# Sharing the unpacking of 4-bit weights anew among three stages of a fused attention and feed-forward kernel

## The chip, the cores and the metric

The kernel runs on one core of a Trainium2 chip. The metric is the device time of one execution in microseconds; the time of a kernel is the median of its runs. The profile is that of one execution, with its own time.

## The reference

The input x has 2 batches of 1024 tokens of 1024 values. It is normalised, and two branches read the result: attention with 32 query heads and 8 key heads of 32 values, causal, with rotary positions; and a gated feed-forward layer of inner width 2752, whose weights come packed as 4-bit numbers with a zero point and a scale for each group of 128 rows. Cut to what matters:

```
xn = layernorm(x)
q, k, v = xn @ wq, xn @ wk, xn @ wv          # q and k are then rotated
s = softmax(causal(q @ k.T / sqrt(32))) @ v @ wo
gate, up = split(xn @ dequant(qweight_gu))   # 1024 x (2 * 2752)
f = (silu(gate) * up) @ dequant(qweight_down)
out = x + s * silu(f)
```

`dequant` is scale times (number minus (zero point + 1)).

## The kernel before

Attention is done for one batch after the other, then the feed-forward layer for both. The order of stages is: layer norm of batch 0; then for each batch a projection to queries, keys and values (`project`), attention (`attend`) and the output projection (`project_out`); then the feed-forward part. The layer norm of batch 1 runs inside the first output projection.

**Unpacking.** TensorE needs the packed weights as floating-point integers. They are unpacked once, written to device memory, and read from there by the feed-forward part. A unit of gate and up is a block of 128 columns of both matrices; there are 22, and the last has 64 columns. The down matrix gives 12 more units. `unpack` is a Python generator that records the instructions of its units in small steps, so that another stage can record them between its own. A unit is four loads on SP's queue (two of packed words, L242, two of zero points, L244), on VectorE an AND (L258), a shift with an AND (L260) and two additions (L263), on ScalarE two conversions to float (L267), and two stores on POOL's queue (L249, 512 KB each). Each `next` on the generator is one turn. It gives one turn for the first load, four for each unit and one for the last store, so n units need 4n + 2 turns. A unit's loads are recorded one unit ahead, and its stores one unit behind.

**Who drives the generator.** Before the change three stages do:
- The first output projection has units 0 to 7, 34 turns. It takes three turns at the start of each part from the eighth of its 14 parts on (21 turns), and the rest after the loop.
- The projection of batch 1 has units 8 to 19, 50 turns. Its inner function `turned` takes three turns after each block of 512 tokens, and there are 20 blocks: 4 of the keys and 16 of the queries.
- The second output projection has units 20 and 21 and the 12 of the down matrix, 58 turns. It takes three turns in each of its 14 parts, 42, and the rest after the loop.

**A block in the projection.** `turned` makes a block of queries or keys with 8 products (L384), and VectorE reads the PSUM bank twice: once times a cosine (L388), once with neighbours swapped (L390). POOL multiplies by the sine and adds (L391, L392). ScalarE then rounds the sum to the high half (L394), VectorE subtracts it for the low half (L396), and SP stores both halves (L397, L398). After each pair of blocks of queries the normalised input is split in the same way (ScalarE L439, VectorE L440) and stored (L441, L442). The turns of `unpack` are recorded under `behind(turn)`, which puts their instructions behind the rotation's last ones.

From the third block pair on, the projection also makes the score products of the first head group (L554, with a mask, L548), whose maximum VectorE takes from PSUM (L564). They use two PSUM banks. After each half of these rows come eight small steps on VectorE (L586 to L591) and four transposes on TensorE (L599), which need them.

**The order of the work.** The stages up to the attention, and the output projection, are recorded in program order, and a scheduler then orders the instructions of each engine; in the attention and in the last product of the feed-forward part the order is written by hand. Each engine executes its own queue in order. So an instruction that waits holds back all that stand behind it on that engine. SP's queue carries nearly all loads and most stores; POOL's carries the stores of unpacked weights and half of those of the output projection, and also the two steps of the rotation.

An output projection has 14 parts in its loop, each 16 products of 128x256 into a PSUM bank (L880), of six in turn. VectorE copies the bank of even parts, ScalarE that of odd ones (L892), and POOL or ScalarE stores the copy (L893). The second output projection runs behind the loads of the whole normalised input (L946) and of the first weights (L937) on SP's queue.

Of the kernel before, what the change touches and what calls it, by code (L numbers as in the profile page):

```python
# [36 lines left out]
def block_kernel(  # L37
# [19 lines left out]
    B, T, D = x.shape  # L57
# [4 lines left out]
    NF = -(-INTER // P)  # L62
# [146 lines left out]
    def look(pool, psp):  # L209

        bad = pool.tile([P, 4], F32, name="bad")
        nc.vector.memset(bad, 0.0)
        yield from survey(pool, bad, sc_gu, qz_gu, gi_gu, z_gu, 0, "gu")
        yield from survey(pool, bad, sc_d, qz_d, gi_d, z_d, 2, "d")
        for g in range(G_GU):
            r0 = g * (P // G_GU)
            r1 = r0 + P // G_GU
            nc.scalar.dma_start(zb_gu[r0:r1], z_gu[g : g + 1].to_broadcast([r1 - r0, 2 * INTER, 2]))
        yield
        for g in range(G_D):  # L220
            r0 = g * 16
            r1 = r0 + 16 if g < G_D - 1 else RD
            nc.scalar.dma_start(zb_d[r0:r1], z_d[g : g + 1].to_broadcast([r1 - r0, D, 2]))
        yield
        scales_turned(pool, psp)
        yield
        one = pool.tile([P, 1], F32, name="one")
        nc.vector.tensor_reduce(one, bad, AX.X, ALU.add)
        ps = psp.tile([1, 1], F32, name="ps_bad", tag="ps")
        nc.tensor.matmul(ps, one, ones_f[:, :1], start=True, stop=True)  # L230
        nc.vector.tensor_scalar(flag, ps, 1.0, None, ALU.min)
        yield
# [126 lines left out]
    def project(b, xnT, w_k, qs, ks, v, side, head):  # L359


        with tc.tile_pool(name="qkv_w", bufs=3, reuse_waits="tile") as wp, tc.tile_pool(name="qkv", bufs=3, reuse_waits="tile") as pool, tc.tile_pool(
# [9 lines left out]
            def behind(turn):  # L372

                order = ExitStack()
                for i in turn:
                    order.enter_context(tc.issue_after(i.ins))
                return order

            def turned(w, dst, work=iter(()), blocks=range(NB)):
                for n in blocks:  # L380
                    tok = slice(n * TB, (n + 1) * TB)
                    ps = psp.tile([P, TB], F32, name="ps_qk")
                    for s in range(NS):
                        nc.tensor.matmul(ps, w[:, s, :], xnT[:, s, tok], start=(s == 0), stop=(s == NS - 1))  # L384
                        if s % 2:
                            next(work, None)
                    t1 = pool.tile([P, TB], F32, name="rot1")
                    nc.vector.tensor_tensor(t1, ps, cs[:, 0, tok], ALU.mult)  # L388
                    t2 = pool.tile([P, TB], F32, name="rot2")
                    nc.vector.stream_shuffle(t2, ps, swap)  # L390
                    nc.gpsimd.tensor_tensor(t2, t2, cs[:, 1, tok], ALU.mult)  # L391
                    turn = [nc.gpsimd.tensor_tensor(t1, t1, t2, ALU.add)]  # L392
                    hi = pool.tile([P, TB], F32R, name="rot_hi", bufs=2)
                    turn.append(nc.scalar.copy(hi, t1))  # L394
                    lo = pool.tile([P, TB], F32R, name="rot_lo", bufs=2)
                    turn.append(nc.vector.tensor_tensor(lo, t1, hi.bitcast(F32), ALU.subtract))  # L396
                    nc.sync.dma_start(dst[0, :, tok], hi.bitcast(F32))  # L397
                    nc.sync.dma_start(dst[1, :, tok], lo.bitcast(F32))  # L398
                    with behind(turn):
                        for _ in range(3 if b else 1):  # L400
                            next(side, None)
                return turn

# [1022 lines left out]
    def start_ffn(stack):  # L1426

        xp = stack.enter_context(tc.tile_pool(name="xs", bufs=1, side="right"))
        xs = [xp.tile([P, NS, T], F32R, name=f"x_{t}") for t in range(2)]
        for _ in activations(xs, 0):  # L1430
            pass
        ring = itertools.cycle([xp.tile([P, D], F32R, name=f"w_{i}") for i in range(6)])
        ws = {(f, u): load_gu(ring, f, u) for f, u in ((0, 0), (0, 1), (1, 0))}
        return xs, ring, ws

    def open_x():
        st = ExitStack()
        xp = st.enter_context(tc.tile_pool(name="x", bufs=1, side="right", reuse_waits="tile"))
        return st, xp.tile([P, NS, T], F32, name="xnT"), xp
# [7 lines left out]
    for b in range(B):  # L1447
        keep_open = ExitStack()
        keep = keep_open.enter_context(tc.tile_pool(name="keep", bufs=1, reuse_waits="tile"))
        oT = keep.tile([P, NS, T], F32, name="oT")  # L1450
        q0_open = ExitStack()
        q0p = q0_open.enter_context(tc.tile_pool(name="at_q0", bufs=1, reuse_waits="tile"))
        with tc.tile_pool(name="at_first", bufs=1, reuse_waits="tile") as fp, tc.tile_pool(
            name="qkv_T", bufs=1, reuse_waits="tile"
        ) as qp:

            room = [q0p.tile([P, T], F32R, name=f"room_{j}") for j in range(1 + 2 * NREP)]
            v = qp.tile([P, NT, N_KV * HD], F32, name="v")
            with tc.tile_pool(name="ps_s", bufs=1, space=PSUM, reuse_waits="tile") as ps_s:
                head = Maxima(qs_dram[b], ks_dram[b], fp, ps_s, room)  # L1460
                if b == 0:
                    with tc.tile_pool(name="prep", bufs=1) as pool, tc.tile_pool(
                        name="prep_ps", bufs=1, space=PSUM
                    ) as psp:
                        first = look(pool, psp)
                        project(b, xnT, w_k, qs_dram[b], ks_dram[b], v, first, head)
                        for _ in first:
                            pass
                else:
                    with tc.tile_pool(name="unpack", bufs=2, side="right", reuse_waits="tile") as up:  # L1470
                        side = unpack(up, range(8, 20), False)
                        project(b, xnT, w_k, qs_dram[b], ks_dram[b], v, side, head)
                        for _ in side:
                            pass
                x_open.close()
                output = Output(b, oT, q0p)
                attend(head, v, oT, output)
        if b == B - 1:
            ffn_args = start_ffn(ffn_open)
            xnT = xp = None  # L1480
        else:
            x_open, xnT, xp = open_x()
        with tc.tile_pool(name="unpack", bufs=3, side="right", reuse_waits="tile") as up:
            side = unpack(up, range(8) if b == 0 else range(20, NF), b == B - 1)
            w_k = project_out(output, side, 3, xnT, xp)
            for _ in side:
                pass
        q0_open.close()
        keep_open.close()
# [57 lines left out]
```

## Time and profile before

| | us |
|---|---|
| median of 3 runs | 2293.89 (2293.84 to 2294.37) |
| the profiled execution, its own time | 2293.33 |
| its span, from the first to the last instruction | 2291.6 |
| TensorE busy in the span | 2239.3 (98%) |
| VectorE busy | 1420.2 (62%) |
| ScalarE busy | 1132.3 (49%) |
| POOL busy | 792.4 (35%) |

The stages around the change in that execution, in us from the start of the span:

| stage | from | to |
|---|---|---|
| first output projection, alone on TensorE but for the transposes of the layer norm | 562 | 668 |
| projection of batch 1 | 668 | 853 |
| attention of batch 1 | 853 | 1191 |
| second output projection, alone on TensorE | 1191 | 1290 |
| feed-forward part | 1290 | 2292 |

A row of the profile's timeline gives the start, the duration, the engine, the line, the operation, what it writes and reads, how many instructions are merged into it, and in brackets how long the engine had stood idle before it and for what. On TensorE a float32 product counts as two records. PE is TensorE, DVE is VectorE, ACT is ScalarE. "Granted clock" (PEclk) is the share of full clock that TensorE was given; it is 1.00 in all stages named here.

### The profile page before, as it was taken

What the parts mean: (1) busy time and instruction counts of PE and PEld (TensorE: products, weight loads), DVE (VectorE), ACT (ScalarE), POOL (GpSimd) and SP (SyncE); (2) the same over time, 40 slices, a digit from 0 to 9 for tenths busy, and PEclk for the clock granted to TensorE, in tenths of its full rate; (3) what the DMA queues carried; (4) which work ended last, traced back from release to release, by engine and by line L of the source; (5) the groups of instructions that cost most, each with busy time, mean ns of one, the idle gap of its engine ahead of it and who ended that gap; (6) DMA issues with size and microseconds to landing.
All of it is one profiled execution on the core that took longest, in us unless ns stands there. A gap on an engine that the chain in (4) does not pass through costs nothing.

```text
span 2291.6 us, 30825 instructions
## 1 busy us (share of the span) xinstructions
PE 2239.3 (98%) x11313; PEld 1537.5 (67%) x11313; DVE 1420.2 (62%) x2268; ACT 1132.3 (49%) x1819; POOL 792.4 (35%) x569
## 2 busy tenths in 40 slices
PE   7989999999999999999999999999999999999998
PEld 4455555555874465555558888888877888888875
DVE  5544677773324736777722367667877777777775
ACT  2102544553223325445533455555887555556875
POOL 1303677774035427776741100000234100001362
PEclk9999999999999999999999999999999999999999
DMA  5727323122468971231319623231846655323475
GB/s 180 220 91 244 80 47 93 38 75 76 129 210 280 301 215 47 52 88 38 80 54 344 181 56 83 55 83 55 303 138 219 176 137 139 96 71 105 137 231 154
DMA packets 262183, 309.50 MB, mean 135 GB/s; under 512 B 19147, under 2 KB 197707, under 8 KB 261880
## 3 DMA queue, kind: packets, MB, share of 16 engines
q1 hardware_dynamic: 245172, 260.62, 38.4%
q0 software_dynamic: 10752, 38.02, 5.2%
q10 hardware_dynamic: 6100, 8.82, 1.2%
q8 instruction: 91, 1.49, 0.3%
q14 instruction: 68, 0.56, 0.1%
HBM read 214.58 MB, written 97.03 MB: 136 GB/s over the span
## 4 chain that ended last, share of the span: by engine, by line
PE 82%; issue 7%; POOL 6%; DVE 2%; ACT 2%; DMA 1%; SPq 0%; ACTq 0%; POOLq 0%; DVEq 0%
PE acc L1198 27%; PE acc L1079 12%; PE ps_wo L880 10%; PE st L661 7%; PE s L554 7%; PE o L708 5%; PE ps_qk L384 5%; PE l L726 3%; PE st L676 2%; PE ps_v L407 1%; POOL rot L391 1%; PE s L548 1%; POOL rot L392 1%; POOL p L821 1%; ACT p L686 1%
## 5 line engine op out<-in xcount | busy, mean ns | idle before, releaser
L1198 PE MATMUL acc<-x,w 128*128 128x512 f32 x2752 | 640.1, 393 | 1.2 <-ACT gate L1169 0.9
L1198 PEld LDWEIGHTS acc<-x,w 128*128 128x128 f32 x2752 | 512.3, 188 | 120.5 <-DVE h L1171 7.2
L564 DVE TENSOR_REDUCE mx<-s 128x1 f32<-128x512 f32 (+3 forms) x672 | 384.8, 608 | 190.3 <-PE s L554 91.7
L968 DVE TENSOR_SCALAR acc<-acc,r_gu 128x1024 f32<-128x1024 f32 x301 | 389.1, 1293 | 166.5 <-PE acc L1198 164.9
L686 ACT ACTIVATE p<-st 128x512 f32<-128x512 f32 (+3 forms) x768 | 314.7, 497 | 316.8 <-PE st L676 314.6
L966 ACT ACTIVATE acc<-acc,r_gu 128x1024 f32<-128x1024 f32 x301 | 327.4, 1088 | 231.5 <-PE acc L1198 226.7
L1182 POOL TENSOR_TENSOR h_lo<-h,h_hi 128x512 fp32r<-128x512 f32 x78 | 100.3, 1287 | 805.2 <-DVE h L1160 300.6
L821 POOL TENSOR_TENSOR p<-p 128x2048 f32<-128x2048 f32 (+3 forms) x122 | 360.0, 2955 | 9.0 <-PE o L708 4.6
L968 DVE TENSOR_SCALAR acc<-acc,r_d 128x512 f32<-128x512 f32 x320 | 241.7, 759 | 62.0 <-PE acc L1079 59.3
L966 ACT ACTIVATE acc<-acc,r_d 128x512 f32<-128x512 f32 x320 | 210.8, 663 | 61.8 <-PE acc L1079 55.0
L384 PE MATMUL ps_qk<-xnT,w_qk 128*128 128x512 f32 x512 | 236.0, 602 | 2.5 <-DVE rot L390 2.5
L880 PE MATMUL ps_wo<-oT,w_o 128*128 128x256 f32 x1024 | 232.1, 382 | 0.0
L1079 PE MATMUL acc<-h_lo,w 128*128 128x512 f32 (+1 forms) x576 | 228.9, 397 | 3.0 <-POOL h_lo L1182 2.6
L1079 PE MATMUL acc<-h_hi,w 128*128 128x512 f32 (+1 forms) x576 | 229.5, 398 | 0.7 <-ACT h_hi L1181 0.7
L880 PEld LDWEIGHTS ps_wo<-oT,w_o 128*128 128x128 f32 x1024 | 191.1, 190 | 40.9 <-issue 16.7
L708 PE MATMUL o<-p,v 128*32 128x512 f32 (+3 forms) x1536 | 162.9, 496 | 0.9 <-POOL p L689 0.9
L384 PEld LDWEIGHTS ps_qk<-xnT,w_qk 128*128 128x128 f32 x512 | 94.6, 192 | 99.8 <-issue 93.4
L689 POOL TENSOR_SCALAR_AFFINE_SELECT p<-p 128x512 f32<-128x512 f32 x128 | 80.5, 636 | 163.5 <-ACT p L686 123.0
L391 POOL TENSOR_TENSOR rot<-rot,cs 128x512 f32<-128x512 f32 x40 | 51.3, 1283 | 239.6 <-DVE rot L390 230.2
L554 PE MATMUL s<-kst,room 128*128 128x512 f32 (+3 forms) x384 | 130.4, 379 | 0.0
L1079 PEld LDWEIGHTS acc<-h_lo,w 128*128 128x128 f32 (+1 forms) x576 | 108.4, 188 | 31.0 <-POOL h_lo L1182 5.4
L1079 PEld LDWEIGHTS acc<-h_hi,w 128*128 128x128 f32 (+1 forms) x576 | 108.3, 188 | 30.6 <-issue 2.9
(163 smaller groups left out, 2405.7 us busy)
## 6 DMA issues: line engine op xcount, KB each, us to landing
w<-ng SPq DMA_DIRECT2D x86, 512.0 KB, 5.2
w<-nd SPq DMA_DIRECT2D x63, 512.0 KB, 4.0
ng<-nf POOLq DMA_DIRECT2D x42, 512.0 KB, 6.9
room<-qs SPq DMA_DIRECT2D x160, 128.0 KB, 4.0
x<-xs SPq DMA_DIRECT2D x32, 512.0 KB, 10.2
qst<-qs SPq DMA_DIRECT2D x96, 128.0 KB, 3.8
xt<-in_L_attn_x SPq DMA_DIRECT2D x16, 512.0 KB, 6.2
w_qk<-in_L_attn_wq SPq DMA_DIRECT2D x16, 512.0 KB, 5.0
```

Source lines behind the costliest of these rows:

```text
L384: nc.tensor.matmul(ps, w[:, s, :], xnT[:, s, tok], start=(s == 0), stop=(s == NS - 1))
L554: nc.tensor.matmul(s[:, c * w : (c + 1) * w], q[j][:, qt * P : (qt + 1) * P], k[:, k0:k1], start=n == 1, stop=c == n - 1 and (n > 1 or not ...
L564: nc.vector.tensor_reduce(mx[:, at, js[0] : js[0] + n, k0 // TB], s[:, : w * n].rearrange("p (j t) -> p j t", j=n), AX.X, ALU.max)
L661: nc.tensor.matmul(s[:, q0:], kst[g][:, kt * P : (kt + 1) * P], stack[g][j][:, qlo + q0 : qlo + TB], start=True, stop=False,)
L686: nc.scalar.activation(p[:, j, q0:], st[j][:, q0:], AF.Exp, scale=1.0 / math.sqrt(HD))
L708: nc.tensor.matmul(o[HD * j : HD * (j + 1), q0:], v[:, kt, HD * g : HD * (g + 1)], p[:, j, q0:], start=(kt == 0), stop=last,)
L821: what(*args)
L880: self.last = nc.tensor.matmul(ps[:, c * self.BLK : (c + 1) * self.BLK], self.ws[c0 + c][:, g, :], self.oT[:, g, t0 : t0 + self.BLK], star ...
L966: nc.scalar.mul(a, a, r)
L968: nc.vector.tensor_scalar(a, a, r, None, ALU.mult)
L1079: nc.tensor.matmul(acc[c], w[:k, c * P : (c + 1) * P], ht[:k, :], start=(f == 0 and t == 0), stop=(t == 1), skip_group_check=(f > 0),)
L1198: nc.tensor.matmul(a[:, n, :], w[i][:, g * P : (g + 1) * P], xs[t][:, g, n * TB : (n + 1) * TB], start=(g == 0 and t == 0), stop=(t == 1), ...
```

## The change

The 22 units of gate and up are shared anew. The first output projection gets units 0 to 10 (11 instead of 8, 46 turns), the projection of batch 1 gets units 11 to 18 (8 instead of 12, 34 turns) and takes two turns a block instead of three, and the second output projection gets units 19 to 21 (3 instead of 2) and the 12 of the down matrix as before (62 turns). The two output projections still take three turns at a time.

```
                     with behind(turn):
-                        for _ in range(3 if b else 1):
+                        for _ in range(2 if b else 1):
                             next(side, None)
...
                     with tc.tile_pool(name="unpack", bufs=2, side="right", reuse_waits="tile") as up:
-                        side = unpack(up, range(8, 20), False)
+                        side = unpack(up, range(11, 19), False)
                         project(b, xnT, w_k, qs_dram[b], ks_dram[b], v, side, head)
...
         with tc.tile_pool(name="unpack", bufs=3, side="right", reuse_waits="tile") as up:
-            side = unpack(up, range(8) if b == 0 else range(20, NF), b == B - 1)
+            side = unpack(up, range(11) if b == 0 else range(19, NF), b == B - 1)
             w_k = project_out(output, side, 3, xnT, xp)
```

## The prediction

> **What bounds the kernel now.** I read the page's busy row first, then the busy time by stretch around the three places that share the unpacking, then TensorE's own waits there, and last the queues that stand behind those waits.
>
> ```profile
> PE 2239.3 (98%) x11313; PEld 1537.5 (67%) x11313; DVE 1420.2 (62%) x2268; ACT 1132.3 (49%) x1819; POOL 792.4 (35%) x569
> ```
>
> TensorE is busy for 98% of the span. A change that adds no matmul can win only what TensorE stands idle, and loses only where it makes TensorE wait anew. So the question is where its 52 us of idle time lie.
>
> ```profile
> core 0: us, PE busy (x) PEld busy (x) DVE busy (x) ACT busy (x) POOL busy (x), PEclk, DMA share, GB/s
> 560.00:668.00 108.00, 108.00 (x543) 94.77 (x536) 34.33 (x83) 31.32 (x49) 20.07 (x26) 1.00 0.68 209
> 668.00:695.00 27.00, 27.00 (x64) 11.96 (x63) 8.64 (x20) 5.60 (x8) 9.25 (x8) 1.00 0.22 71
> 695.00:853.00 158.00, 152.03 (x468) 83.55 (x467) 83.36 (x184) 42.89 (x61) 61.81 (x56) 1.00 0.88 274
> 1165.00:1290.00 125.00, 125.00 (x638) 100.26 (x637) 26.46 (x69) 37.40 (x53) 27.98 (x30) 1.00 0.75 247
> ```
>
> The rows are the first output projection, the start of the second projection, the rest of it, and the second output projection. Both output projections keep TensorE fully busy. All the idle time that the change can reach is in the third row: 158.00 - 152.03 = 5.97 us, 0.26% of the span, with the DMA engines at 0.88. That caps the gain at about 6 us. TensorE's rows with a wait in that stretch are these, the wait in brackets:
>
> ```profile
> 755.68 0.51 PE L554 MATMUL s<-room,room 128*128 128x512 f32 x1 [1.23 <-DVE mx L564]
> 762.19 0.38 PE L599 MATMUL m_ps<-ident_b,mt 128*128 128x128 bf16 x4 [0.62 <-DVE mt L588]
> 782.63 0.50 PE L554 MATMUL s<-room,room 128*128 128x512 f32 x1 [0.99 <-DVE mx L564]
> 790.88 0.44 PE L554 MATMUL s<-room,room 128*128 128x384 f32 x1 [0.19 <-DVE mx L564]
> 800.55 0.50 PE L554 MATMUL s<-room,room 128*128 128x512 f32 x1 [1.38 <-DVE mx L564]
> 820.03 0.38 PE L599 MATMUL m_ps<-ident_b,mt 128*128 128x128 bf16 x4 [1.47 <-DVE mt L588]
> ```
>
> They sum to 5.88 us. Each is a score product (L554) that needs a PSUM bank which a maximum on VectorE (L564) has yet to read, or the transposes (L599) that need the last step after those maxima (L588). VectorE is not full (83.36 of 158 us): the maxima stand in its queue behind something. For the third wait its timeline shows what:
>
> ```profile
> 779.81 0.69 DVE L396 TENSOR_TENSOR rot_lo<-rot,rot_hi 128x512 fp32r<-128x512 f32 x1 [3.06 <-ACT rot_hi L394]
> 780.42 0.29 DVE L260 TENSOR_SCALAR nib<-qw 128x512 uint16<-128x512 uint16 x1
> 780.62 0.69 DVE L440 TENSOR_TENSOR x_lo<-xnT,x_hi 128x512 fp32r<-128x512 f32 x1
> 781.22 0.42 DVE L263 TENSOR_TENSOR nib<-nib,zt 128x512 uint16<-128x512 uint16 x1
> 781.55 0.69 DVE L440 TENSOR_TENSOR x_lo<-xnT,x_hi 128x512 fp32r<-128x512 f32 x1
> 782.16 0.75 DVE L564 TENSOR_REDUCE mx<-s 128x1 f32<-128x256 f32 x2
> ```
>
> After a wait of 3.06 us for the rotation to come back from ScalarE, half a unit (L260, L263) and two splits (L440) run before the maximum that TensorE waits for.
>
> **The change: what a unit costs.** A full unit of gate and up is on VectorE 0.29 + 0.29 + 2 x 0.42 = 1.42 us (L258, L260, L263), on ScalarE 2 x 1.06 = 2.1 us (L267), on POOL 2 x 0.91 = 1.8 us of issuing stores (L249, 512 KB each), on SP four loads of some 0.44 us (L242, L244, 64 KB each). Nothing of it is added or taken away in all; 22 units stay. Three places get other numbers.
>
> **First output projection, 8 to 11 units.** Sums added: VectorE 4.3, ScalarE 6.3, POOL 5.4, SP 5.3 us. Engine time isn't what paces them: the last conversions start at 637.88, 642.27, 646.34 and 651.52, 4.55 us apart, with the DMA engines at 1.0. Three more end at 653.5 + 3 x 4.55 = 667.2. In the built program they stand on ScalarE between the copies of the last three parts, on VectorE before the copy of the last even part, on POOL before its store.
>
> ```profile
> 651.52 2.00 ACT L267 ACTIVATE nf<-nib 128x1024 fp32r<-128x1024 uint8 x2 [3.17 <-DVE nib L263]
> 667.98 0.58 ACT L892 COPY wo_r<-ps_wo 128x512 f32<-128x512 f32 x1 [13.23 <-PE ps_wo L880]
> 1277.35 2.00 ACT L267 ACTIVATE nf<-nib 88x1024 fp32r<-88x1024 uint8 x2 [4.97 <-DMA nd<-nf]
> 1290.12 0.59 ACT L892 COPY wo_r<-ps_wo 128x512 f32<-128x512 f32 x1 [8.95 <-PE ps_wo L880]
> ```
>
> ScalarE waited 13.23 us for TensorE before its last copy, so 13.6 us of units fill that gap and no more. Next on these queues is the first rotation: VectorE's L388 at 674.85, ScalarE's L394 at 678.97. The cover is 7.6 us and more. SP loses its own: the second projection's first loads wait for the last stores (before: 659.88 and 663.28), come 13.6 us later, at some 677, and behind them stands the first key store at 679.61. Even some us late that costs nothing, as two rotation buffers, 6.9 us apart, lie behind it. I put this part at 0; without its cover it costs 1 for 1 from 7.6 us on.
>
> **Second projection, 12 to 8 units, 3 turns a block to 2.** Four units less: VectorE 5.7, ScalarE 8.5, POOL 7.3, SP 7 us, and 4 x 1.25 MB = 5 of 43 MB less in transfers. Only what stands ahead of a maximum counts. I read the built program's order on VectorE at each wait:
> - 782.63: the order is now L396, L260, L263, L564, L440 twice. The maximum ends 0.20 + 0.34 + 0.42 = 0.96 us after 780.42, at 781.4; TensorE was ready at 782.63 - 0.99 = 781.64. The 0.99 goes.
> - 800.55: L258, L260, L263 twice and L440 twice stood between L396 (to 797.46) and the maximum; now L260, L263. It ends near 798.8, TensorE was ready at 799.17. The 1.38 goes. In both places the next maximum comes after the two L440, 2.6 to 2.8 us behind L396, and is needed 2 us after the first: covered by 0.5.
> - 790.88: L258 and L263 no longer delay the rotation at 783.82. The 0.19 goes.
> - 820.03: nothing changes in the queue (L396, L440 twice, L564 twice, the eight small steps). The 1.47 stays.
> - 755.68 and 762.19, the end of the first half's maxima: here the order turns against the change. TensorE's first product of the second half now follows 62 query matmuls instead of 64, the transposes 68 instead of 70. A matmul is 0.863 us (32 in 27.63), so 1.73 us of cover is gone. VectorE's queue up to L588 has one L440 (0.60) and an L258/L263 pair (0.71) less, 1.31. Net 0.42 more wait: 1.85 becomes 2.27. Bounds: +1.73 if VectorE gains nothing there; -1.85 if both waits vanish.
>
> The rule weighed here: the row of L263 in this stretch,
>
> ```profile
> L263 DVE TENSOR_TENSOR nib<-nib,zt x21: 407/418/1497, 694.4 to 798.4; 128x512 uint16<-128x512 uint16 x21
> ```
>
> has a largest time 1.08 us above its median, and one L440 has 0.98 us. The Trainium skill ("SBUF — State Buffer", section "Who interferes with whom") says that a VectorE instruction with two SBUF inputs and a GpSimd one that reads SBUF exclude each other whole: the later one waits. Both long ones do start beside L391 or L392 on POOL, and both lie ahead of the first two waits. POOL runs those two for 2.5 of some 8 us a block, so by the rule about a third of the L263 would be hit: eight fewer of them would save 8 x 0.32 x 0.6 = 1.6 us of VectorE time, but any L440 or L263 that the new order puts beside a rotation can bring a new us ahead of a maximum. By the row it is 1 in 21, so 0.4 us. I take the row, and leave both ends in the range: -2.1 or +1.0 us at the first two waits.
>
> **Second output projection, 2 units of gate and up to 3 (12 of the down matrix stay).** Its first unit runs before the load of x as before; the added one comes with the tail unit after 1224. Conversions from 1231.11 to 1277.35 are 12 steps of 3.85 us, so the last ends at 1279.35 + 3.85 = 1283.2. Behind it on ScalarE are the copies of the last two odd parts, and for those banks TensorE waits in the feed-forward part, at 1289.73. Cover 10.4 us, 6.5 left: cost 0. The weight loads issued from 1265.77 come some 4 us later; the DMA engines fall idle by 1294 and those weights are needed after 1312.
>
> **Sum.** -0.99 - 0.19 - 1.38 + 0.42 = -2.14 us. The profiled execution took 2293.33 us (span 2291.6 and 1.7 around it), so 2291.2; the median of the runs is 2293.89, 0.56 above, so the forecast is 2291.8.
>
> **Rivals.**
> - The whole wait goes: the first two waits vanish as well, and with less traffic the last. 2293.89 - 4.41 to - 5.88: 2288.0 to 2289.5. For it: DMA at 0.88, and L396 and L439 waiting on stores. Against: the last queue is unchanged.
> - Given back: the first two waits grow by the full 1.73 and a new collision (1.0), which leaves 2293.89 - 2.56 + 2.73 = 2294.1. For it: VectorE is busy 16.7 of 20 us between 740 and 760. This is also what it looks like if the change does nothing.
> - Slower: the added unit in the second output projection. The DMA engines are at 0.98 to 1.03 there, and the last conversions already sit 7.0 us apart. It decides from 10.4 us of delay; each further us is paid whole. If the added unit costs two such steps, 14 us, it ends 3.6 us late: 2295.4; three steps, 10.6 late: 2302.4. Against it: 12 steps averaged 3.85.
>
> **How the numbers follow.** Forecast 0.52 (its own range 2290.3 to 2293.2), given back 0.22 (2293.2 to 2296), whole wait 0.12, slower 0.14 (2296 and up). The range 2288.8 to 2297.2 leaves out about half of the fast case and most of the slow one, some 0.15. A measurement of this kernel can tell about 0.2% (4.6 us) from no change: faster than 2289.3 is most of the fast case, 0.09; slower than 2298.5 the far part of the slow one, 0.10; within, 0.81.
>
> **What would show it.** Right: no wait near the three later products, some 1.5 us before the second transposes, 2 to 2.5 us in all at the end of the first half; last conversion of the first output projection near 667, of the second near 1283. Wrong: a TensorE wait within 20 us of either output projection's end, or new L554 waits behind an L440 or L263 of over 1 us.

## The result, and the profile after

The changed kernel takes 2304.24 us (median of 6 runs, 2300.55 to 2306.41) where the kernel before takes 2293.93 (6 runs, 2293.48 to 2294.84): a ratio of 1.0043, with a 95% interval of 1.003 to 1.0056. It is 10 us slower. The forecast was 2291.8, the range ended at 2297.2.

The profiled execution took 2300.55 us with a span of 2298.4, against 2293.33 and 2291.6 before. It is the fastest of the six, so it shows only 6.8 us of the loss; other profiles (below) have to show the rest. First the page's busy row:

```profile
PE 2242.1 (98%) x11313; PEld 1538.2 (67%) x11313; DVE 1419.2 (62%) x2268; ACT 1130.8 (49%) x1819; POOL 791.9 (34%) x569
```

TensorE has the same 11313 instructions and is 2.8 us longer at them. The busy time in the four stretches of the prediction (each row: the stretch, its length, the busy time of TensorE, of its weight loads, of VectorE, ScalarE and GpSimd, TensorE's granted clock, the share of the DMA engines, GB/s):

```profile
560.00:668.00 108.00, 108.00 (x537) 94.72 (x537) 37.91 (x95) 35.20 (x52) 21.80 (x26) 1.00 0.66 206
668.00:695.00 27.00, 27.00 (x65) 11.93 (x64) 5.27 (x13) 4.67 (x6) 8.46 (x10) 1.00 0.68 193
695.00:853.00 158.00, 148.87 (x442) 79.68 (x441) 80.38 (x176) 36.08 (x55) 58.88 (x52) 0.98 0.78 238
1165.00:1290.00 125.00, 125.00 (x652) 97.72 (x649) 32.07 (x76) 43.15 (x62) 31.70 (x31) 1.00 0.71 238
```

Both output projections still fill TensorE. The start of the second projection has three times the DMA traffic it had (0.68 for 0.22): the end of the first output projection hangs over into it. The third row lost what the change was to win: TensorE is busy 148.87 us for 152.03, and its clock is no longer 1.00. TensorE's rows with a wait:

```profile
728.85 0.44 PE L554 MATMUL s<-room,room 128*128 128x128 f32 x1 [4.71 <-DMA room<-qs]
766.84 0.38 PE L599 MATMUL m_ps<-ident_b,mt 128*128 128x128 bf16 x4 [0.60 <-DVE mt L588]
770.14 0.50 PE L554 MATMUL s<-room,room 128*128 128x512 f32 x1 [2.00 <-DVE mrow L601]
825.27 0.38 PE L599 MATMUL m_ps<-ident_b,mt 128*128 128x128 bf16 x4 [1.60 <-DVE mt L588]
...
1299.77 19.52 PE L1198 MATMUL acc<-x,w 128*128 128x512 f32 x84 [1.44 <-ACT acc L966]
```

The three waits that were to go (0.99, 0.19, 1.38 us) are gone, and so is the one of 1.23. Three others came: 2.00 us right behind the transposes (L554 for L601); 4.71 us at the first score product of all, which has no wait in the kernel before, for the loads of the query stack (the queries in the layout in which the score products take them), and 1.44 us at the start of the feed-forward part. After the 4.71 us TensorE runs slowly for a while (stretches of 5 us, the clock is the third number from the end):

```profile
725.00:730.00 5.00, 1.15 (x2) 0.71 (x3) 2.57 (x6) 1.06 (x2) 2.10 (x2) 0.78 1.01 266
730.00:735.00 5.00, 5.00 (x9) 2.30 (x8) 2.55 (x5) 2.08 (x3) 2.09 (x3) 0.53 1.03 277
735.00:740.00 5.00, 5.00 (x14) 2.23 (x13) 1.34 (x3) 0.62 (x1) 1.08 (x1) 1.00 1.01 366
```

Busy time times what is missing of the clock gives the price, as an estimate: 1.15 x 0.22 + 5.00 x 0.47 = 2.6 us. The length of the stage agrees with it: from the first product of the projection (L384) to the first value product (L407) it is 163.61 us for 157.67, 5.9 us more, of which the waits are 3.0. The sum for this execution: waits in the second projection 8.91 for 5.88, +3.0; clock +2.6; feed-forward start +1.4; together 7.1, against 6.8 in the span (this execution was 0.7 us ahead when the second projection began: 667.09 for 667.78).

Why is the query stack late? The queues behind the first output projection, by engine (ScalarE, GpSimd, SyncE):

```profile
670.44 2.00 ACT L267 ACTIVATE nf<-nib 128x1024 fp32r<-128x1024 uint8 x2 [7.32 <-DMA ng<-nf]
672.35 0.57 ACT L892 COPY wo_r<-ps_wo 128x512 f32<-128x512 f32 x1
683.59 0.37 ACTq L893 DMA_DIRECT2D sT<-wo_r  x1
686.99 0.62 ACT L394 CAST rot_hi<-rot 128x512 fp32r<-128x512 f32 x1 [14.07 <-POOL rot L392]
...
661.87 0.73 POOL L893 DMA_DIRECT2D sT<-wo_r  x1 [12.31 <-DVE nib L258]
662.60 5.26 POOL L249 DMA_DIRECT2D ng<-nf  x6
672.74 1.72 POOL L249 DMA_DIRECT2D ng<-nf  x2 [4.88 <-ACT nf L267]
674.27 0.88 POOL L893 DMA_DIRECT2D sT<-wo_r  x1
683.36 0.98 POOL L497 MEMSET mt<- 128x512 bf16 x2 [8.21 <-DMA sT<-wo_r]
684.36 1.26 POOL L391 TENSOR_TENSOR rot<-rot,cs 128x512 f32<-128x512 f32 x1
...
678.85 1.57 SPq L242 DMA_DIRECT2D qw<-in_L_ffn_qweight_gu  x2
687.64 0.32 SPq L397 DMA_DIRECT2D ks<-rot_hi  x1
```

And GpSimd's queue in the kernel before:

```profile
653.13 0.73 POOL L893 DMA_DIRECT2D sT<-wo_r  x1 [2.77 <-DVE wo_r L892]
...
662.06 0.72 POOL L893 DMA_DIRECT2D sT<-wo_r  x1 [6.44 <-DVE wo_r L892]
665.91 0.98 POOL L497 MEMSET mt<- 128x512 bf16 x2 [3.13 <-DMA qw<-in_L_ffn_qweight_gu]
...
676.33 1.27 POOL L391 TENSOR_TENSOR rot<-rot,cs 128x512 f32<-128x512 f32 x1 [9.39 <-issue]
```

It starts on VectorE. Its copy of the last even part but one came at 660.48 (651.74 before), because steps of units stood ahead of it and waited for their loads. GpSimd's store of that part waited 12.31 us for it, and the stores of three units were held up behind this store; then six went out at once. So the last conversion found its buffer occupied for 7.32 us and ended at 672.4. GpSimd's last store was issued at 674.27 (662.06 before) and landed 9.0 us later beside the backlog (3.8 before). Only then could the memsets run, which clear the tiles for the shifts of the softmax. They have no input; they waited because they take over the memory from which this store reads. (Before, the row names a load, but the last store landed at the same time, 662.06 + 3.8 = 665.9.) Behind the memsets on the same queue stands the first rotation: 684.36, where it was 676.33.

### The profile page after: what moved, and what is told of

Same layout as the page of the kernel before. It is cut to its first block, busy times and chain, and to the rows that moved or that the text cites. A ratio compares the mean times of both kernels' runs of the same rounds, so it can differ in the third digit from the quotient of the medians.

```text
span 2298.4 us, 30826 instructions
## 1 busy us (share of the span) xinstructions
PE 2242.1 (98%) x11313; PEld 1538.2 (67%) x11313; DVE 1419.2 (62%) x2268; ACT 1130.8 (49%) x1819; POOL 791.9 (34%) x569
## 4 chain that ended last, share of the span: by engine, by line
PE 77%; issue 8%; POOL 7%; DMA 3%; DVE 2%; ACT 2%; SPq 0%; ACTq 0%; POOLq 0%; DVEq 0%
PE acc L1198 27%; PE acc L1079 12%; PE ps_wo L880 8%; PE st L661 7%; PE s L554 7%; PE o L708 5%; PE l L726 3%; PE ps_qk L384 2%; PE st L676 2%; POOL rot L391 2%; POOL rot L392 2%; PE ps_v L407 1%; PE s L548 1%; POOL p L821 1%; ACT p L686 1%
## 5 line engine op out<-in xcount | busy, mean ns | idle before, releaser
L966 ACT ACTIVATE acc<-acc,r_gu 128x1024 f32<-128x1024 f32 x301 | 327.4, 1088 | 232.3 <-PE acc L1198 227.5
L966 ACT ACTIVATE acc<-acc,r_d 128x512 f32<-128x512 f32 x320 | 210.8, 663 | 61.8 <-PE acc L1079 55.1
L384 PE MATMUL ps_qk<-xnT,w_qk 128*128 128x512 f32 x512 | 238.8, 608 | 2.5 <-DVE rot L390 2.5
L384 PEld LDWEIGHTS ps_qk<-xnT,w_qk 128*128 128x128 f32 x512 | 95.4, 194 | 100.8 <-issue 94.6
L394 ACT CAST rot_hi<-rot 128x512 fp32r<-128x512 f32 x40 | 24.6, 617 | 229.2 <-POOL rot L392 200.2
L554 PE MATMUL s<-kst,room 128*128 128x512 f32 (+3 forms) x384 | 130.5, 379 | 0.0
```

What stands on the lines that cost most here:

```text
L554: nc.tensor.matmul(s[:, c * w : (c + 1) * w], q[j][:, qt * P : (qt + 1) * P], k[:, k0:k1], start=n == 1, stop=c == n - 1 and (n > 1 or not ...
L966: nc.scalar.mul(a, a, r)
```

## The experiments

All times are medians, beside runs of the kernel before on the same chip; the ratio is given with its 95% interval. Where a ratio's interval holds 1.0, the kernel's time is not told apart from that of before.

| kernel | units (first output projection, second projection, second output projection) | us | before | ratio |
|---|---|---|---|---|
| changed, again | 11, 8 in 2 turns, 3 | 2303.06 | 2294.52 | 1.0045 (1.0028 to 1.0062) |
| first output projection alone | 11, 9 in 3 turns, 2 | 2299.30 | 2294.13 | 1.0026 (1.0015 to 1.0037) |
| second projection alone | 8, 8 in 2 turns, 2 (4 left out) | 2293.49 | 2294.13 | 0.9997 (0.9988 to 1.0005) |
| second output projection alone | 8, 11 in 3 turns, 3 | 2294.84 | 2294.13 | 1.0000 (0.9992 to 1.0009) |
| changed, memsets later | 11, 8 in 2 turns, 3 | 2297.82 | 2294.13 | 1.0019 (1.0012 to 1.0026) |
| changed, memsets and loads later | 11, 8 in 2 turns, 3 | 2300.81 | 2294.52 | 1.0033 (1.0021 to 1.0045) |
| changed, units begun earlier | 11 early, 8 in 2 turns, 3 | 2295.74 | 2294.52 | 1.0006 (0.9998 to 1.0013) |
| the same with 12 and 2 | 12 early, 8 in 2 turns, 2 | 2293.28 | 2294.52 | 0.9996 (0.9987 to 1.0004) |
| 10 units, late | 10, 10 in 3 turns, 2 | 2293.36 | 2294.47 | 0.9999 (0.9990 to 1.0008) |
| second output projection alone, 6 buffers | 8, 11 in 3 turns, 3 | 2293.39 | 2294.47 | 0.9997 (0.9988 to 1.0005) |
| best | 11 early, 9 in 3 turns, 2 | 2290.57 | 2294.47 | 0.9979 (0.9969 to 0.9988) |

### The three parts, each alone

Theory A: the end of the first output projection is late, and the second projection starts late on GpSimd. Theory B: the new turns of the second projection put stores ahead of the loads of the query stack. The first output projection alone, against the kernel before:

```
-                        side = unpack(up, range(8, 20), False)
+                        side = unpack(up, range(11, 20), False)
...
-            side = unpack(up, range(8) if b == 0 else range(20, NF), b == B - 1)
+            side = unpack(up, range(11) if b == 0 else range(20, NF), b == B - 1)
```

> The first output projection alone gets 11 units; the second projection keeps its 3 turns a block with the 9 units that are left (11 to 19), the second output projection its 2. Theory A (the 11-unit end of the first output projection holds the first rotations of the second projection back, and the query stack for the first score product comes late): the first rotation again starts on GpSimd at about 684 us, TensorE waits 4 us or more at the first score product, and the time is 2299 to 2305. Theory B (the turns of the second projection, shared anew, put the stores of the first split ahead of the loads of the query stack on SyncE, and that makes the stall): no wait of over 1 us there, 2293 to 2295.

It has half of the loss, +5.2 us, and the whole stall. TensorE's wait there:

```profile
730.73 0.45 PE L554 MATMUL s<-room,room 128*128 128x128 f32 x1 [5.96 <-DMA room<-qs]
```

The first rotation was at 685.2. Theory A holds, and B falls with the next one, the second projection alone (the edit is against the changed kernel; units 8 to 11 are not unpacked, so this kernel leaves out a part of the work):

```
-    ng_dram = [dram.tile([2, D, P], F32, name=f"ng_{f}", tag=f"ng_{f}") for f in range(NF)]
+    ng_dram = [dram.tile([2, D, P], F32, name=f"ng_{f}", tag=f"ng_{f}") for f in range(NF)]; ng_dram[8:12] = ng_dram[12:16]
...
-                        side = unpack(up, range(11, 19), False)
+                        side = unpack(up, range(12, 20), False)
...
-            side = unpack(up, range(11) if b == 0 else range(19, NF), b == B - 1)
+            side = unpack(up, range(8) if b == 0 else range(20, NF), b == B - 1)
```

> The second projection alone gets the change: 8 units in 2 turns a block (12 to 19). The first output projection keeps 8 and the second 2; units 8 to 11 are not unpacked at all, and the feed-forward part reads units 12 to 15 in their place. Theory A: no stall at the first score product, the three waits of 2.56 us go as predicted, 2291.0 to 2292.5. Theory B: a stall of 2 us or more at the first score product, 2296 or more.

No stall at the first score product, although the stores of the first split (from 714.92) do stand ahead of the loads of the query stack (from 717.60) here. TensorE's waits in the second projection, and the clock around the second of them:

```profile
759.64 0.38 PE L599 MATMUL m_ps<-ident_b,mt 128*128 128x128 bf16 x4 [0.60 <-DVE mt L588]
762.94 0.80 PE L554 MATMUL s<-room,room 128*128 128x512 f32 x1 [2.00 <-DVE mrow L601]
821.06 0.38 PE L599 MATMUL m_ps<-ident_b,mt 128*128 128x128 bf16 x4 [1.61 <-DVE mt L588]
```

```profile
760.00:765.00 5.00, 3.00 (x7) 1.28 (x5) 2.88 (x7) 2.60 (x4) 2.85 (x3) 0.72 0.80 240
765.00:770.00 5.00, 5.00 (x13) 2.95 (x12) 2.12 (x5) 0.00 (x0) 0.00 (x0) 0.59 1.02 338
```

The waits are 4.21 us for 5.88, so 1.67 won; but the 2.00 us wait is followed by a low clock, 3.00 x 0.28 + 5.00 x 0.41 = 2.9 us, which more than takes it back in this execution, the slowest of its twelve. The median stands 0.6 us below before, inside its interval; the expected 2291.0 to 2292.5 was missed.

The second output projection alone, against the kernel before:

```
-                        side = unpack(up, range(8, 20), False)
+                        side = unpack(up, range(8, 19), False)
...
-            side = unpack(up, range(8) if b == 0 else range(20, NF), b == B - 1)
+            side = unpack(up, range(8) if b == 0 else range(19, NF), b == B - 1)
```

> The second output projection alone gets the change, 3 units of gate and up for 2; the second projection keeps 3 turns a block with the 11 units 8 to 18, the first output projection its 8. If the 1.44 us wait at the first feed-forward product belongs to the added unit, it shows here again and the time is 2295.0 to 2296.0. The step as it was predicted (cost 0): no such wait, 2293.4 to 2294.4.

The median lies between the two expectations and does not decide. The profile shows the wait again. TensorE and ScalarE around the start of the feed-forward part:

```profile
1291.73 1.20 PE L1198 MATMUL acc<-x,w 128*128 128x512 f32 x4 [1.17 <-ACT wo_r L892]
1295.36 21.84 PE L1198 MATMUL acc<-x,w 128*128 128x512 f32 x84 [2.43 <-ACT acc L966]
...
1291.09 0.59 ACT L892 COPY wo_r<-ps_wo 128x512 f32<-128x512 f32 x1 [7.62 <-DMA sT<-wo_r]
```

3.6 us of waits that the kernel before does not have, in an execution of 2298.79 us, the slowest of its twelve. The last copy waited 7.62 us until an earlier part's store had landed and freed its buffer.

### The links of the late end

The memsets of the shift tiles out of the rotations' way (against the changed kernel):

```
-            for mt in self.mts:
-                nc.gpsimd.memset(mt, 0.0)
...
-            nc.gpsimd.memset(self.mxs[0][:, :, :, 1], MASKED)
...
                 if c == 0:
+                    with behind(turn): [nc.gpsimd.memset(t, x) for t, x in [(mt, 0.0) for mt in head.mts] + [(head.mxs[0][:, :, :, 1], MASKED)]]
                     head.queries()
```

> The changed kernel, with the three memsets of the shift tiles moved on GpSimd's queue from ahead of the first rotation to behind the second one of the first query block; they keep their wait for the store of the last copy, but no rotation stands behind it. If they are the link that holds the rotations (they waited 8.21 us, to 683.36): the first rotation starts on GpSimd at about 676, the stall at the first score product goes, 2292 to 2295. If the loads on SyncE (from 678.85, ahead of the first key store) or the backlog of the DMA queues hold the query stack back by themselves: the rotation is early but the stall stays 2 us or longer, 2297 to 2304.

The first rotation ran at 676.4, as hoped, but the time and the stall, 2.28 us for 4.71, are those of the second expectation: the memsets are one link and not the only one. The second rotation still waited, until 688.4: ScalarE's last store came only at 684.54, and the rounding of the first rotation behind it at 685.05. The suspects are the loads on SyncE (the first at 679.92), which stand ahead of the first key store. They were put behind the key stores as well:

```
-                    nc.sync.dma_start(dst[1, :, tok], lo.bitcast(F32))
+                    turn.append(nc.sync.dma_start(dst[1, :, tok], lo.bitcast(F32)))
```

> The changed kernel with both links between the late end and the first rotations cut: the memsets of the shift tiles behind the second rotation of the first query block, and the loads of the second projection's units behind the key stores on SyncE. If these two links are the whole chain: ScalarE's last store right behind its copy near 673, the first two rotations on GpSimd near 676 and 683, no wait for the query stack of over 0.5 us at the first score product, 2294 to 2297. If the DMA queues alone make the key and query stacks late: a stall of 2 us or more there still, 2297 to 2302.

ScalarE's store now comes right behind its copy, at 674.31, and the first key store at 680.02; so those loads had held it (what ScalarE's store waits for, the trace does not name). But there is a third link. VectorE, GpSimd and TensorE:

```profile
687.38 0.29 DVE L258 TENSOR_SCALAR nib<-qw 128x512 uint16<-128x512 uint16 x1 [4.57 <-DMA qw<-in_L_ffn_qweight_gu]
...
688.40 1.35 POOL L391 TENSOR_TENSOR rot<-rot,cs 128x512 f32<-128x512 f32 x1 [9.06 <-DVE rot L390]
...
727.13 0.30 PE L554 MATMUL s<-room,room 128*128 128x128 f32 x1 [1.90 <-DMA room<-qs]
```

On VectorE the first unit of the second projection stands ahead of the second rotation's shuffle, and its load waits for the late end too. With both links cut the second rotation is still where it was, and 1.90 us of stall stay. The time, 2300.81, lies in the range of the second expectation and the stall just below it; what holds the second rotation is a load that VectorE's queue waits for. Why this kernel's median is above that of the one with the memsets alone was not settled (the intervals touch, on two chips).

If every engine has a piece of the late end in its queue, then only an earlier end helps:

```
-                    if g == 0 and (xnT is None or i >= NT - 1):
+                    if g == 0 and (xnT is None or i >= NT - 4):
```

> The changed kernel (11, 8, 3 units), with the units of the first output projection begun three parts of its loop earlier, so that the last ones are over sooner. Theory A (the late end is the cause): first rotation on GpSimd at 676 to 678, no wait for the query stack at the first score product, 2293.5 to 2297.5, what is left being the added unit of the second output projection and the 2 us wait for the row of shifts. Rival (11 units are too much for that stage wherever they start): TensorE waits in the stage itself, between 600 and 667, or the stall stays, 2299 or more.

The group of first rotation steps on GpSimd (its first and last start are the two times):

```profile
L391 POOL TENSOR_TENSOR rot<-rot,cs x12: 1257/1263/1267, 676.4 to 759.1; 128x512 f32<-128x512 f32 x12
```

The rotation is back at 676.4, the query stack is not waited for (0.24 us in a second profile), and of 8.5 us 1.2 are left. TensorE stayed full from 560 to 668 with the 11 units. So 11 units are not too many for the stage; their late end makes the stall. With the third unit of the second output projection taken away as well:

```
-                        side = unpack(up, range(11, 19), False)
+                        side = unpack(up, range(12, 20), False)
...
-            side = unpack(up, range(11) if b == 0 else range(19, NF), b == B - 1)
+            side = unpack(up, range(12) if b == 0 else range(20, NF), b == B - 1)
```

> 12 units in the first output projection begun three parts earlier, 8 in the second projection in 2 turns a block, 2 in the second output projection as before. If the two failed steps are the end of the first output projection and the added unit of the second, both are gone and the gain of the second projection alone is left: 2291.5 to 2294.5. If the twelfth unit brings the lateness back: a stall at the first score product and 2298 or more.

2293.28, inside the first range, and no wait at the start of the feed-forward part: the second failed step is gone too.

How sharp is the edge? 10 units, begun as late as in the kernel before (against that kernel):

```
-                        side = unpack(up, range(8, 20), False)
+                        side = unpack(up, range(10, 20), False)
...
-            side = unpack(up, range(8) if b == 0 else range(20, NF), b == B - 1)
+            side = unpack(up, range(10) if b == 0 else range(20, NF), b == B - 1)
```

> 10 units in the first output projection, begun as late as in the kernel before, 10 in the second projection in 3 turns a block, 2 in the second output projection. By the theory of the late end: 11 units set the first rotation back by 8 us, each unit is worth about 4 of it, so it comes some 4 us late, and the wait for the query stack, 4.5 to 6 us with 11, is 0 to 2 us: 2293 to 2297. If each added unit costs its share of the +5.2 us (no threshold): about +3.5, 2297 to 2299.

The first rotation came at 679.4, 3.1 us late, and the wait was

```profile
725.00 0.30 PE L554 MATMUL s<-room,room 128*128 128x128 f32 x1 [1.14 <-DMA room<-qs]
```

with the clock at 1.00 behind it. The time is that of before. So there is an edge between 10 and 11 units, but it is not a cover of 7.6 us: 3 us of lateness cost about 1, and 8 us cost 4.5 to 6 and the clock. What softens it is that late rotations follow each other faster: in the changed kernel the first ones come 5.97 us apart on GpSimd, 6.87 before, so that the lateness shrinks from 8.0 us at the first to 3.8 at the sixth (714.45 for 710.62).

### Buffers at the second output projection

Six buffers for the copied parts in place of four, on top of the kernel with the second output projection alone:

```
-            res = st.enter_context(tc.tile_pool(name="wo_out", bufs=4, reuse_waits="tile"))
+            res = st.enter_context(tc.tile_pool(name="wo_out", bufs=4 if xnT is not None else 6, reuse_waits="tile"))
```

> The second output projection alone with 3 units, as in the earlier run, and with 6 buffers for the copied parts there instead of 4. If the waits at the first feed-forward products (1.17 and 2.43 us in that run) come from copies that wait for a buffer until its store has landed: they go, 2292 to 2294. If they come from the queues of ScalarE and GpSimd, in which the last copies and stores stand behind the units: they stay, 2294 to 2297.

```profile
1293.74 19.48 PE L1198 MATMUL acc<-x,w 128*128 128x512 f32 x84 [1.01 <-ACT acc L966]
```

ScalarE's last copy no longer waits for a buffer, but for TensorE's products:

```profile
1290.00 0.59 ACT L892 COPY wo_r<-ps_wo 128x512 f32<-128x512 f32 x1 [4.63 <-PE ps_wo L880]
```

With that the wait for the copy (1.17 us) is gone. The other wait, for L966, is 1.01 us here for 2.43; but with four buffers and a third unit it is anything from 0.90 to 2.43 in the profiles, so how much of it was the buffer stays open. The times of the two kernels (0.9997 and 1.0000 of before) don't differ by more than their intervals.

### What differs between executions

The first profiled execution of the changed kernel is the fastest of its six. How do the slower ones lose more?

> The changed kernel as it is, once more beside the variants below. If its 10 us are the sum of what the parts cost when done alone (about +5.2 for the first output projection, -0.6 for the second projection, +0.7 for the second output projection), it is some 5 us slower than before, near 1.002; if the parts make each other worse, 8 to 12 us again. Theory of the clock: where TensorE waits 2 us or more its granted clock shows about 0.5 for some 5 us behind the wait in most profiles, and not in all, so the place of the loss differs from the first profile of this kernel.

The loss came back whole, 8.5 us, at 1.0045. The ratios of the parts alone sum to 1.0026 - 0.0003 + 0.0000 = 1.0023; their three intervals together give about 0.0017 either way, so the whole is above the sum, but not surely. The profiled execution, again the fastest, took 2300.23, with 4.49 us at the first score product and, unlike the first profile, a low clock behind the 2.00 us wait (0.66 from 770 to 775). Further profiles of it, and of the kernel with early units:

> The changed kernel again, for one profile. If the slower executions differ by the clock alone: the waits are the known ones (about 4.6 at the first score product, 2.0 at the row of shifts, 1.4 to 3.6 at the first feed-forward products), and each us above 2300 is matched by time at a granted clock near 0.5 behind one more of them. If they differ by their waits: the wait for the query stack or at the first feed-forward products is 2 us or more longer than in the first profile.

> The same kernel and the same question as in the look before it; two looks, since one may fall on a fast execution.

> The variant with early units again, for one more profile. By the clock theory: an execution at 2295 or below shows no granted clock below 1 behind the 2.0 us wait near 763 or behind the waits near 1296; one at 2297 or above shows it in at least one of the two places. By the rival, an execution of the fast group has waits shorter by 3 us or more in all.

One of the changed kernel took 2301.57 us with waits of 4.91, 2.01 and 1.00. The next took 2305.62; TensorE and the clock at its feed-forward start:

```profile
1299.91 1.19 PE L1198 MATMUL acc<-x,w 128*128 128x512 f32 x4 [1.08 <-ACT wo_r L892]
1302.41 21.05 PE L1198 MATMUL acc<-x,w 128*128 128x512 f32 x84 [1.31 <-ACT acc L966]
```

```profile
1300.00:1305.00 5.00, 3.69 (x11) 2.63 (x12) 1.12 (x2) 2.09 (x2) 0.00 (x0) 0.79 0.59 193
1305.00:1310.00 5.00, 5.00 (x20) 4.04 (x20) 2.82 (x3) 2.36 (x3) 0.00 (x0) 0.87 0.03 12
```

Here the added unit costs 2.4 us of waits and 3.69 x 0.21 + 5.00 x 0.13 = 1.4 us of clock, where the first profile had 1.44 and nothing: 2.4 of the 5.4 us between the two spans. The rest is spread: 1.1 us were there at the first value product (141.8 for 140.7), 1.7 came after the last gate and up product. So neither expectation is met alone: waits and clock both vary, and not in one place. The kernel with early units took 2294.01 for the 2299.51 of its first profile. Both have the 2.00 us wait for the row of shifts; in the first the clock fell to 0.77 and 0.54 behind it, in this one it stayed at 1.00, which is 3.0 of the 5.5 us. About 2.5 were there before 535 us. At the feed-forward start this one had a low clock too (0.71), which the expectation excluded.

### A version that beats both

Early units, the second projection left at 3 turns, the second output projection left at 2 units:

```
-                    if g == 0 and (xnT is None or i >= NT - 1):
+                    if g == 0 and (xnT is None or i >= NT - 4):
...
-                        side = unpack(up, range(8, 20), False)
+                        side = unpack(up, range(11, 20), False)
...
-            side = unpack(up, range(8) if b == 0 else range(20, NF), b == B - 1)
+            side = unpack(up, range(11) if b == 0 else range(20, NF), b == B - 1)
```

> Made to keep what the second projection gains and neither loss: 11 units in the first output projection begun three parts of its loop earlier, 9 in the second projection still in 3 turns a block (in the run of the first output projection alone that left waits of 1.23, 0.63 and 1.45 us there, without the 2 us wait for the row of shifts), 2 in the second output projection. By the waits: 5.88 - 3.31 = 2.6 us less than before, no granted clock below 1 between 668 and 1330: 2291 to 2293. If early units cost something of their own: no difference.

2290.57 us, 0.9979 of before (0.9969 to 0.9988), 0.4 us below the expected range. TensorE's waits in the second projection:

```profile
756.17 0.50 PE L554 MATMUL s<-room,room 128*128 128x512 f32 x1 [1.22 <-DVE mx L564]
762.68 0.38 PE L599 MATMUL m_ps<-ident_b,mt 128*128 128x128 bf16 x4 [0.62 <-DVE mt L588]
817.35 0.38 PE L599 MATMUL m_ps<-ident_b,mt 128*128 128x128 bf16 x4 [1.45 <-DVE mt L588]
```

and the stretch they stand in:

```profile
695.00:853.00 158.00, 154.55 (x485) 85.65 (x483) 80.65 (x174) 39.22 (x59) 56.77 (x50) 1.00 0.80 254
```

3.29 us of waits for 5.88, with three units less and the turns unchanged, no wait of 2 us, and the clock at 1.00. So a gain of the predicted size was there to be had, by fewer units in the second projection, begun early in the first output projection; the turns could stay. 2.6 of the 3.9 us between the medians are these waits. The profiled execution is the slowest of its ten, and its span is only 0.8 us below that of before: it is 2.5 us ahead when the feed-forward part begins, and loses 1.7 us by the end, 1.8 of them in waits for the weights of the down matrix that the profile of before does not have. Other kernels show 0.2 to 1.1 us there; what makes them was not looked for.

## Why the prediction was wrong

- **"I put this part at 0" (first output projection).** This is the step that failed: +5.2 us alone, the largest loss of the three parts. Three links of its argument broke.
  - "Three more end at 653.5 + 3 x 4.55 = 667.2": the last ended at 672.4. The pace was read while GpSimd's stores flowed. It does not hold once a store of a copied part stands 12.31 us in that queue and six unit stores follow at once.
  - "Next on these queues is the first rotation": GpSimd's memsets stood ahead of it, at 665.91 in the trace of before, and wait for the last store to land. ScalarE's last store was held back by the loads on SyncE, and VectorE's first unit waited for such a load; these loads came late, too. I asked when the engines would be done, and not what memory the next work takes over, and from whom.
  - "Even some us late that costs nothing, as two rotation buffers, 6.9 us apart, lie behind it": the rotation buffers are not what TensorE needs first. Six rotations in a row feed the key and query stacks, and their end met the first score product without a wait in the kernel before, which is no sign of slack. 3.1 us of lateness already gave a wait of 1.14.
- **"The 0.99 goes", "the 1.38 goes", "the 0.19 goes"**: right, in every kernel with 2 turns; but with 9 units they go in 3 turns as well (first output projection alone, and the best), so the smaller number of units is enough. "The 1.47 stays": 1.60.
- **"Net 0.42 more wait: 1.85 becomes 2.27"**: 2.60, so the sum was near, but by luck, as neither part of it came. The wait of 1.23 us went altogether. The 0.62 stayed at 0.60, and a new wait of 2.00 us came one product later: the product behind the transposes waits for the copy of the row (L601), which stands on VectorE behind a rotation that is waiting for ScalarE. It is in all ten profiles with 2 turns a block and in none of the six with 3. So the second projection alone brings 0.6 us (by its interval, from 2.8 us less to 1.1 more) for the predicted 2.14.
- **"Cover 10.4 us, 6.5 left: cost 0" (second output projection).** The date was right: the last conversion was forecast to end at 1283.2 and ended at 1283.0 when this part was changed alone. The cover was not: the last copy waited 7.62 us for a buffer until a store had landed, and the stores issued behind the conversion on GpSimd took long, 12.7 us for the unit's and some 13 for each of two parts. There are 0.9 to 3.9 us of waits in all kernels with a third unit, though the median of this part alone does not show a loss. The slower rival named the place and put the edge at 10.4 us of delay; it is much nearer.
- **"I take the row" (the rule that was weighed)**: the runs agree with the rule, and it mattered at one of the two waits. Two rows of the kernel before, then all L440 and L263 of this stretch in the changed one:

```profile
752.61 1.27 POOL L392 TENSOR_TENSOR rot<-rot,rot 128x512 f32<-128x512 f32 x1
752.76 2.27 DVE L440 TENSOR_TENSOR x_lo<-xnT,x_hi 128x512 fp32r<-128x512 f32 x2 [1.02 <-ACT x_hi L439]
```

```profile
L440 DVE TENSOR_TENSOR x_lo<-xnT,x_hi x16: 681/684/685, 719.2 to 836.8; 128x512 fp32r<-128x512 f32 x16
L263 DVE TENSOR_TENSOR nib<-nib,zt x15: 414/424/426, 694.5 to 804.3; 128x512 uint16<-128x512 uint16 x15
```

  In all six profiles with 3 turns one L440 takes 1.67 us for 0.68, and one L263 1.50 for 0.42. Of all L263, L396 and L440 in this stretch only these two run beside the rotation's steps on GpSimd. In the ten profiles with 2 turns none runs beside them, and none is long. The long L440 ends right before the maximum for which TensorE waited 1.23 us, and this wait is gone with it: about 1 us, the saving end of the range. The order changed as well, and no run separates the two. The new collision at the other end did not come, and without the long L263 the second wait stayed.
- **The sum had no line for the clock.** A wait was taken at its length. The wait of 4.71 us cost 7.3.
- "Wrong: a TensorE wait within 20 us of either output projection's end": this sign came for the second. For the first the damage showed 61 us behind the end, so the sign was set too close.

## What to carry to other kernels

When work is added to the end of a stage, follow its last store, not its last arithmetic: ask which memory that store frees, what is first to take that memory over on every queue, and what the next stage's first consumer needs through the whole chain, even 50 us later. A consumer that shows no wait may have no slack at all; unless the trace shows when its input landed, put a price on lateness. And work that may hang over an end is better begun earlier in the stage that has room than cut finely at its end.

## What the runs showed of the hardware

TensorE's granted clock fell for some 5 us behind short waits, to 0.5 where it was lowest. Of 10 waits of 2.0 us for the row of shifts, in ten profiles, 6 were followed by a low clock, at a price of 1.1 to 3.0 us each (busy time times what is missing of the clock); all 5 waits of over 4 us were, at 1.6 to 2.9 us; between these, 1.90 us was and 2.28 us was not; between 660 and 1330 us no wait of 1.64 us or less that stood alone was. The trace of before had it already, behind a wait of 1.94 us in the first half of the kernel:

```profile
225.30 0.47 PE L554 MATMUL s<-kst,qst 128*128 128x128 f32 x2 [1.94 <-DMA qst<-qs]
```

```profile
225.00:230.00 5.00, 4.70 (x26) 4.14 (x26) 3.22 (x7) 1.64 (x4) 0.85 (x2) 0.70 1.03 231
```

The Trainium skill ("TensorE: Matmul & The Clock Gate", section "What's actually happening") has the clock at half after an idle window of about 3.4 us, in windows that run freely. That it is now one and now the other for the same 2.0 us wait fits free windows; that 2 us are enough does not fit a window that must be idle throughout, and the runs decide: count a wait of 2 us on TensorE in this kernel as 2 us and, more often than not, some 2 more.

The store of a copied part (256 KB) on GpSimd took 2.6 us to land at the end of the first output projection of the changed kernel, and 9.0 beside the backlog of unit stores; two took some 13 us each at the end of the second.

A VectorE step with two inputs in on-chip memory took about 1 us longer where it ran beside a rotation step on GpSimd: 1.67 us for 0.68 (L440), 1.50 for 0.42 (L263).
